# Third layer's self-attention: where the steps of its second half stand in the slots of the loop beside it

## The chip, the cores and the metric

The kernel runs on one core of a Trainium2 chip, in one launch. The metric is the device time of one execution in microseconds (us). A core has five engines that each work through an instruction list of their own in order: TensorE (PE, matrix products), VectorE (DVE), ScalarE (ACT), GpSimd (POOL) and SyncE (SP, which here only starts transfers). They meet through semaphores: an instruction waits until another engine has counted far enough. An instruction that waits holds up everything behind it on its own engine.

## The reference

The input `x` is 16 batch rows of 56 tokens by 256 features; a context of 1500 rows by 128 features goes with each batch row. Four layers run one after the other on `x`, each with attention to the context:

```python
x = L0(x, ctx)                      # one-head attention, a gate, rmsnorm
x = L1(x, ctx, mask)                # layernorm, 16-head cross attention, then a gelu MLP
x = L2(x, ctx, types, positions)    # self-attention, cross attention, then a silu MLP
x = L3(x, ctx, mask)                # as L1, other weights
```

The change is in the self-attention of the third layer (L2). Cut to what matters, with 16 heads of 16 features, and with two sets of weights ("v" and "l") between which a mask `vm` of the tokens chooses:

```python
x = rms_norm(hidden, ln_in_w)
mixed = where(vm, x @ v_qkv, x @ l_qkv)
q, k, v = heads(split(mixed, 3))
q, k = apply_rotary(q, k, position_ids)
p = softmax(where(causal, q @ k.T / 4, lowest))
ctx = p @ v
hidden = hidden + where(vm, ctx @ v_dense, ctx @ l_dense)
ci = rms_norm(hidden, ln_post_cross_w)       # then the cross attention to the 1500 context rows
```

## The kernel before, in words

**Groups and items.** The 16 batch rows make four groups of four (`gi` 0 to 3, `T` = 224 tokens). A layer on a group is an item; `program` runs 16 items in order, `k` = 0 to 15. An item's main loop (`att0`, `att13`, `att2`) does the attention to the context. Everything else (what comes before an item's attention, `pre...`, and after it, `post...`) is written as Python generators that run beside the main loop of another item: the main loop takes a step of the generator now and then, and the instructions of that step are recorded at that place. So `pre2(gi)`, which holds the changed lines, runs beside item `k` = 7 + `gi`: for group 0 beside the last attention of the second layer (`rows`), for groups 1 to 3 beside the cross attention of the third layer (`att2`) of the group before.

**What sets how many steps a slot takes.** A generator yields the TensorE time that its step is worth, or nothing ("an empty turn"). `pace(share, kept, most)` adds `share` to a balance `line["due"]` and takes up to `most` steps while the balance is over `kept`; each step's worth is taken off. An empty turn ends the call at once, and leaves the balance (up to 3.0) for the next one. `pace` returns whether it took a step that was worth something, and `att2` uses that:

```python
weights_pair(b, j)
full = pace(SHARES[gi][line["behind"]], -0.8, 1)
...
if ahead < B and full:
    largest(ahead, n_ahead)
if last >= 0:
    sums_chunk(last, n)
    sums_chunk(last, n + 1)
if ahead < B and not full:
    largest(ahead, n_ahead)
```

A slot of `att2` is one `j` of six for each batch row `b`. In it stand `weights_pair` (L1441 spreads the shifts into four banks, L1450 adds the scores to them; ACT takes the exponentials `pw` out of these banks at L1455, POOL adds them up at L1467), `largest` (L1404, four banks; DVE takes the largest out of each at L1409), `sums_chunk` (L1482), in some slots `own_sums` (L1508), `values` (L1387), `keys` (L1375) or `shifts` (L1417 to L1430), and a second call of `pace` at the end that takes up to two steps.

**The self-attention's steps.** `scores(pr)` makes the scores of half `pr` (two batch rows) in two banks `e`, and ACT takes exponentials into a tile `s`. `weights(pr, e)` divides `s` by its sums, on DVE alone (L1178, L1179, L1180). `turns(pr, e)` turns a tile by 16 small products with the identity (L1188) and copies it on ACT to `turned` (L302). `sums(pr)` needs both tiles of a half: 16 products with `v` (L1205), then ACT's `own` (L302) and DVE's L1216 into `cT`. With both halves done, DVE masks `cT` twice (L1322), and PE multiplies by the two value matrices (L1329, the value product), whose sum DVE adds to `x` (L1335). The squares of `x` follow on ACT (L389), the root and the scaled rows `xn` on POOL (L390, L320, L400), and PE turns `xn` (L310).

**Banks.** Every product but the long sums goes to one ring of seven banks of PSUM, the memory that PE writes to: `ps_s`, tag "sc", `bufs=7`. The tiles take the banks in turn, in the order in which the program asks for them, so a product waits until the reader of the tile seven places earlier is done.

**Order.** The program is recorded in the order of these calls; the tile framework then orders each engine's list, and may move an instruction past others.

Of the kernel before, what the change touches and what calls it, by code (L numbers as in the profile page):

```python
# [62 lines left out]
def tile_kernel(ctx: ExitStack, tc: tile.TileContext, a, layers=4, groups=NG):  # L63
# [18 lines left out]
    def psum(pool, tag):  # L82
        return pool.tile([128, 512], F32, tag=tag, name=tag)
# [5 lines left out]
    def mm():  # L89
        return psum(ps_s, "sc")  # L90
# [1131 lines left out]
    def pre2(gi):  # L1222
# [12 lines left out]
        scores, weights, turns, sums = self_attention(qT, kept, v, cT)  # L1235
# [68 lines left out]
        weights(0, 1)  # L1304
        turns(0, 0)
        yield 1.2
        weights(1, 0)
        turns(0, 1)
        yield 1.2
        weights(1, 1)  # L1310
        sums(0)
        yield 0.7
        turns(1, 0)
        yield 1.2
        turns(1, 1)
# [4 lines left out]
        for n, m in enumerate((vm, nvm)):  # L1320
            mrow = m[:, gi * G : (gi + 1) * G, :].rearrange("p b n -> p (b n)")
            nc.vector.tensor_tensor(  # L1322
                ce[:, n], cT, mrow.unsqueeze(1).to_broadcast([128, 2, T]), ALU.mult
            )
        p = mm()
        for i in range(NT):
            for n in range(2):
# [365 lines left out]
    def program():  # L1693
# [5 lines left out]
        for name in ("L1", "L3"):  # L1699
            parts.append(tuple(partial(f, name) for f in (pre13, first13, att13, post13)))  # L1700
        parts.insert(2, (pre2, first2, att2, None))
        items = [(*parts[l], gi) for l in range(layers) for gi in range(groups)]
        states = {}
# [335 lines left out]
```

## Time and profile before

| what | value |
|---|---|
| three runs | 1436.54, 1442.94, 1444.49 us; median 1442.94 us |
| the profiled execution | 1437.15 us; its span from first to last instruction 1435.3 us |
| busy share of the span | PE 95%, DVE 54%, ACT 52%, POOL 37% |
| mean granted TensorE clock | 0.986 |
| PE idle before L1329, waiting for L1322 | 6.8 us in 4 waits |
| PE idle before L1188, waiting for L1180 | 4.6 us in 3 waits |
| PE idle before L1205, waiting for `turned` | 2.8 us in 2 waits |

The page of the profile gives busy times by engine and by group of instructions; its answers on waits give, for each line of an engine, what it waited for, in total, how often, and at most. A timeline gives the start, the length and the count of each group in order, with the idle time ahead of it in brackets. An fp32 product shows as two records, so 16 products of L1188 are "x32". L302 is the line of a helper that copies on ACT; the tile's name tells which copy it is. The granted clock says at which part of its full speed TensorE ran in a stretch.

### The profile page before, as it was taken

What the parts mean: (1) busy time and instruction counts of PE and PEld (TensorE: products, weight loads), DVE (VectorE), ACT (ScalarE), POOL (GpSimd) and SP (SyncE); (2) the same over time, 40 slices, a digit from 0 to 9 for tenths busy, and PEclk for the clock granted to TensorE, in tenths of its full rate; (3) what the DMA queues carried; (4) which work ended last, traced back from release to release, by engine and by line L of the source; (5) the groups of instructions that cost most, each with busy time, mean ns of one, the idle gap of its engine ahead of it and who ended that gap; (6) DMA issues with size and microseconds to landing.
All of it is one profiled execution on the core that took longest, in us unless ns stands there. A gap on an engine that the chain in (4) does not pass through costs nothing.

```text
span 1435.3 us, 32417 instructions
## 1 busy us (share of the span) xinstructions
PE 1357.3 (95%) x13638; PEld 938.2 (65%) x13638; DVE 777.7 (54%) x1794; ACT 744.8 (52%) x1703; POOL 526.2 (37%) x567
## 2 busy tenths in 40 slices
PE   6989999999899999999999999999899998999998
PEld 4667677775656556655555556656467776877776
DVE  4444754647575754467545755455565445455641
ACT  2334866756543547445554544444356565557661
POOL 0011001010101677767767768788743112100000
PEclk9999999999999999999999999999999999999998
DMA  7853224232322021110201022131122343333320
GB/s 270 351 191 126 85 89 145 90 112 65 103 76 81 23 82 52 54 56 24 81 31 43 29 71 68 52 103 56 39 82 94 134 152 101 124 118 123 108 89 10
DMA packets 38808, 135.78 MB, mean 95 GB/s; under 512 B 8605, under 2 KB 18493, under 8 KB 34557
## 3 DMA queue, kind: packets, MB, share of 16 engines
q1 hardware_dynamic: 33901, 119.03, 24.1%
q0 software_dynamic: 2592, 10.85, 2.2%
q10 hardware_dynamic: 2160, 3.74, 0.8%
q8 instruction: 109, 1.79, 0.5%
q14 instruction: 46, 0.38, 0.1%
HBM read 129.01 MB, written 4.59 MB: 93 GB/s over the span
## 4 chain that ended last, share of the span: by engine, by line
PE 75%; DVE 12%; ACT 6%; POOL 3%; DMA 3%; issue 1%; SPq 0%; DVEq 0%; POOLq 0%; ACTq 0%
PE sc L642 9%; PE sc L624 8%; PE sc L1092 7%; PE sc L1404 7%; PE sc L1450 4%; PE o L1482 4%; PE sc L1642 4%; DVE mx L1409 3%; PE sc L907 3%; PE sc L1120 3%; PE sc L1387 3%; PE sc L1441 3%; PE sc L1661 2%; PE sc L1375 2%; POOL all L1467 2%; ACT p L302 2%
## 5 line engine op out<-in xcount | busy, mean ns | idle before, releaser
L1467 POOL TENSOR_TENSOR all<-all,pw 125x448 f32<-125x448 f32 x300 | 341.1, 1149 | 125.8 <-ACT pw L1455 114.7
L1409 DVE TENSOR_REDUCE mx<-sc 112x1 f32<-112x500 f32 x384 | 233.4, 669 | 140.6 <-PE sc L1404 140.5
L1455 ACT ACTIVATE pw<-sc 125x448 f32<-125x448 f32 x384 | 177.7, 550 | 102.8 <-PE sc L1450 100.1
L631 ACT ACTIVATE p<-p,few 128x384 f32<-128x384 f32 x224 | 136.9, 611 | 99.3 <-DVE few L627 98.9
L624 PE MATMUL sc<-ktl,qa 128*128 128x384 f32 x448 | 176.9, 504 | 0.0
L627 DVE CUSTOM_DVE_ANT_0 p<-sc,mkl 128x384 f32<-128x384 f32 x224 | 121.8, 551 | 92.1 <-PE sc L624 87.4
L642 PE MATMUL sc<-p,kvl 32*128 32x224 f32 x2160 | 149.5, 353 | 4.7 <-DVE qa L940 3.3
L642 PEld LDWEIGHTS sc<-p,kvl 32*128 32x128 f32 x2160 | 136.3, 185 | 20.5 <-issue 9.6
L642 PE MATMUL o<-p,kvl 32*128 32x224 f32 x720 | 144.6, 352 | 0.0
L143 POOL TENSOR_SCALAR mkl<-m32l 128x384 bf16<-128x384 uint8 x32 | 16.3, 510 | 314.1 <-DVE few L627 292.5
L642 PEld LDWEIGHTS o<-p,kvl 32*128 32x128 f32 x720 | 130.7, 185 | 0.0
L302 ACT ACTIVATE p<-p,few 128x384 f32<-128x384 f32 x224 | 121.1, 608 | 8.6 <-DVE few L618 7.2
L1404 PE MATMUL sc<-ck,qs 32*112 32x500 f32 x768 | 122.5, 626 | 2.8 <-ACT ck L302 1.4
L661 DVE STREAM_TRANSPOSE p<-p 128x768 f32<-128x768 f32 (+1 forms) x96 | 102.8, 1095 | 28.6 <-ACT p L302 28.4
L624 PEld LDWEIGHTS sc<-ktl,qa 128*128 128x128 f32 x448 | 78.8, 190 | 37.4 <-issue 9.0
L1450 PE MATMUL sc<-qs,ck 32*125 32x224 f32 x1536 | 98.8, 355 | 0.0
L320 POOL TENSOR_TENSOR stat<-stat,half_less 112x2 f32<-112x2 f32 (+1 forms) x33 | 23.1, 700 | 201.8 <-DVE stat L344 162.0
L302 ACT ACTIVATE ot<-sc 128x224 f32<-128x224 f32 x64 | 32.0, 609 | 121.1 <-PE o L642 83.5
L1482 PE MATMUL o<-pw,vc 125*32 125x224 f32 x1536 | 93.0, 359 | 0.0
L1482 PEld LDWEIGHTS o<-pw,vc 125*32 125x32 f32 x1536 | 40.2, 109 | 69.9 <-issue 57.2
L1450 PEld LDWEIGHTS sc<-qs,ck 32*125 32x125 f32 x1536 | 77.4, 183 | 1.1
L302 ACT ACTIVATE vc<-sc 125x512 f32<-125x512 f32 x48 | 28.6, 596 | 82.0 <-PE sc L1387 79.2
(286 smaller groups left out, 2360.7 us busy)
## 6 DMA issues: line engine op xcount, KB each, us to landing
kvl<-in_ctx_last SPq DMA_DIRECT2D x30, 768.0 KB, 4.2
kt<-in_ctxT SPq DMA_DIRECT2D x23, 750.0 KB, 5.0
w<-in_L_W SPq DMA_DIRECT2D x16, 1024.0 KB, 4.8
w<-in_L_Wq SPq DMA_DIRECT2D x8, 1024.0 KB, 5.0
w<-in_L_Wo SPq DMA_DIRECT2D x8, 1024.0 KB, 5.6
ktl<-in_ctxT SPq DMA_DIRECT2D x32, 192.0 KB, 2.5
w<-in_L_v_qkv SPq DMA_DIRECT2D x4, 768.0 KB, 6.8
w<-in_L_l_qkv SPq DMA_DIRECT2D x4, 768.0 KB, 4.1
```

Of the source, the lines that this page charges most:

```text
L302: nc.scalar.activation(out, in_, AF.Copy, scale=scale)
L624: line["scored"] = nc.tensor.matmul(sc[:, :LW], u["q"][:, i * 128 : (i + 1) * 128], u["kt"], start=True, stop=True).ins.name
L627: line["drained"] = nc.vector.tensor_tensor_reduce(u["p"][:, i], sc[:, :LW], u["mask"], 1.0, -LOWEST, ALU.add, ALU.min, mn[:, i : i + 1],) ...
L631: nc.scalar.activation(u["p"][:, i], u["p"][:, i], AF.Exp, bias=mn[:, i : i + 1], scale=-1.0, accum_out=den[:, i : i + 1],)
L642: product = nc.tensor.matmul(o[g][:, : RB * BW], y["kv"][part, j, :], y["p"][part, :, j * BW : (j + 1) * BW], start=j == 0, stop=j == LB - ...
L661: nc.vector.transpose(blocks, blocks)
L1404: nc.tensor.matmul(banks[g][: 2 * N, :SW], made["q"][part, rows], made["k"][part, cols], start=True, stop=True,)
L1409: line["drained"] = nc.vector.tensor_reduce(made["mx"][:, half * 4 + g, s : s + 1], banks[g][: 2 * N, :SW], AX.X, ALU.max).ins.name
L1450: nc.tensor.matmul(banks[g][:CP, c * QH : (c + 1) * QH], made["k"][part, at : at + CP], made["q"][part], start=False, stop=c == 1, skip_gr ...
L1455: line["weighed"] = nc.scalar.activation(p[:, :, g * QH : (g + 1) * QH], banks[g][:CP, : 2 * QH].rearrange("p (c n) -> p c n", c=2), AF.Ex ...
L1467: added = engine.tensor_tensor(made["all"][:, cols], made["all"][:, cols] if j else p[:, 0, cols], p[:, c, cols], ALU.add,)
L1482: nc.tensor.matmul(made["o"][part, :QH], made["v"][:, n, part], p[:, r * QH : (r + 1) * QH], start=n == 0, stop=n + 1 == NC, skip_group_ch ...
```

## The change

In `pre2`, behind the first turn of the first half, the second half's first weighting `weights(1, 0)` goes and an empty turn stands in its place, ahead of the first half's second turn. Both weightings of the second half come one step later. A second empty turn stands between the halves, behind `weights(1, 1)`, and a third ahead of the value product, behind the two masked copies. No instruction is added or taken away. Line numbers in this document are those of the kernel before; in the changed kernel the lines below the change stand three further down.

```diff
         weights(0, 1)
         turns(0, 0)
         yield 1.2
-        weights(1, 0)
+        yield
         turns(0, 1)
         yield 1.2
-        weights(1, 1)
+        weights(1, 0)
         sums(0)
         yield 0.7
+        weights(1, 1)
+        yield
         turns(1, 0)
         yield 1.2
         turns(1, 1)
...
             nc.vector.tensor_tensor(
                 ce[:, n], cT, mrow.unsqueeze(1).to_broadcast([128, 2, T]), ALU.mult
             )
+        yield
         p = mm()
         for i in range(NT):
             for n in range(2):
```

## The prediction

> **What bounds the kernel now.** The first line of the page's busy part says who sets the time:
>
> ```profile
> PE 1357.3 (95%) x13638; PEld 938.2 (65%) x13638; DVE 777.7 (54%) x1794; ACT 744.8 (52%) x1703; POOL 526.2 (37%) x567
> ```
>
> PE idles only 1435.3 − 1357.3 = 78.0 us. A change that adds and drops no instruction can win only idle time of PE, or time that PE spent at a lower clock. So I read PE's waits next, for the lines that the change moves:
>
> ```profile
> PE sc L1329 <- DVE l L1322: 6.8, 4, 1.8
> PE sc L1188 <- DVE s L1180: 4.6, 3, 1.6
> PE sc L1205 <- ACT turned L302: 2.8, 2, 2.1
> ```
>
> Each row is total, number of waits, longest. They are 14.2 us, 1.0% of the span: the most that could go in waits. L1329 waits once in each group; L1188 once in groups 1 to 3, L1205 twice in group 0 (beside `rows`). The third view is PE's timeline in group 1 (groups 2 and 3 repeat it within 0.1 us, but for the clock):
>
> ```profile
> 498.30 0.93 PE L1450 MATMUL sc<-qs,ck 32*125 32x224 f32 x16
> 500.74 1.14 PE L1188 MATMUL sc<-ident,s 120*64 120x56 f32 x32 [1.51 <-DVE s L1180]
> 501.81 1.11 PE L1404 MATMUL sc<-ck,qs 32*112 32x500 f32 x8
> ...
> 505.21 0.71 PE L1441 MATMUL sc<-shift,ones_r 2*125 2x448 f32 x4
> 505.52 1.16 PE L1450 MATMUL sc<-qs,ck 32*125 32x224 f32 x16
> 506.61 0.61 PE L1205 MATMUL sc<-turned,l 56*32 56x112 f32 x32
> ...
> 517.35 0.61 PE L1205 MATMUL sc<-turned,l 56*32 56x112 f32 x32
> 517.90 0.96 PE L1482 MATMUL o<-pw,vc 125*32 125x224 f32 x16
> 520.52 1.98 PE L1329 MATMUL sc<-w,l 128*112 128x256 f32 x8 [1.66 <-DVE l L1322]
> ```
>
> The reader sees two holes, 1.51 and 1.66 us, and between them dense work. The fourth view, DVE's timeline there, shows who is late:
>
> ```profile
> 500.07 2.09 DVE L1180 TENSOR_TENSOR s<-s,stat 120x448 f32<-120x448 f32 x2
> 502.09 0.60 DVE L1178 TENSOR_REDUCE stat<-s 120x8 f32<-120x448 f32 x1
> 502.73 0.20 DVE L1179 RECIPROCAL stat<-stat 120x8 f32<-120x8 f32 x1
> 502.97 0.68 DVE L1180 TENSOR_TENSOR s<-s,stat 120x448 f32<-120x448 f32 x1
> 503.57 2.42 DVE L1409 TENSOR_REDUCE mx<-sc 112x1 f32<-112x500 f32 x4
> 505.91 0.49 DVE L1514 RECIPROCAL rest<-sc 128x56 f32<-128x56 f32 x1
> ```
>
> DVE has no gap from the weightings to L1409, which empties the four banks of L1404. The last view is the clock by stretches (the number before the last two is the granted clock):
>
> ```profile
> 820.00:821.00 1.00, 0.94 (x20) 0.57 (x13) 1.00 (x3) 0.40 (x1) 0.00 (x0) 1.00 0.00 0
> 821.00:822.00 1.00, 0.00 (x0) 0.00 (x0) 1.00 (x5) 0.95 (x3) 0.00 (x0) 1.00 0.00 0
> 822.00:823.00 1.00, 0.50 (x16) 0.50 (x17) 1.00 (x2) 0.90 (x3) 0.83 (x1) 0.94 0.00 0
> 823.00:824.00 1.00, 1.00 (x22) 0.99 (x19) 1.00 (x2) 0.00 (x0) 0.92 (x2) 0.50 0.00 0
> ```
>
> This is group 3's hole before L1188 (1.56 us): half clock follows. From that turn to L1205 takes 7.16 us (822.50 to 829.66) instead of 5.87 in group 2 (664.29 to 670.16): a price of 1.3 us. In group 0 half clock also follows the holes of 2.13 and 1.82 us, from about 379.3 to 382.7, which costs half of 3.4 = 1.7.
>
> **The change in the order.** The changed program's instruction lists differ from the old ones only at these four places; no transfer moves, on SP or another queue. In groups 1 to 3 DVE's list keeps its order up to the value product, third weighting ahead of L1409, although the call comes later in the source. What moves is PE: the second turn of half 0 goes from ahead of L1404 to behind L1387, a slot's end; L1482 comes ahead of L1404, since an empty turn makes `pace` return false; the turns of half 1 go a piece later, so that the last one stands right ahead of its L1205; L1329 moves behind L1482, L1404, L1424 and L1375. ACT's copies follow their turns. POOL's list changes in groups 1 and 2 alone: the second L320 stands ahead of L400.
>
> **Groups 1 and 2, walked with group 1's times.** PE is free at 499.23. L1482 0.90, L1404 1.04, L1508 0.51, L1387 1.07 end at 502.75, the turn (1.07) at 503.82; its tile is ready at 502.16. The 1.51 us hole is gone here. But the ring of seven banks now gives L1441 exactly the four banks of this slot's L1404; before, it was the turn's and three of them. So its fourth product waits for the fourth L1409, at 505.99, with 0.2 us from DVE's end to PE's start (L1514 ends at 506.40, L1205 starts at 506.61). L1450 (0.86) runs from 506.27 to 507.13, against 506.61 before: **0.5 lost**, the hole having moved two products on. L1455 follows 1.0 us behind the start of L1450 and frees the next L1404's banks; that start moves more than that end, so **0.15 more is lost**. The last turn ends at about 517.97; ACT starts 0.19 later (512.11 to 512.30 shows this), copies in 0.54, and 0.2 us of L1205 and L1441 is there to fill: **0.65 lost** on `turned`, until 518.85. Then **1.66 won**: L1329 needs `own` (0.6), L1216 (0.57) and both L1322 (1.16), 2.5 us behind L1205 with delays, and 4.6 us of L1441, L1450, L1482, L1404, L1424 and L1375 lie between. With L1404's DVE work early, L1441's next wait (0.36) and the stretched L1450 (1.15 for 0.86) go: **0.65 won**. Last, L1335 now ends at 528.45 instead of 526.3: squares 0.91, L390 0.2, L320 0.72, the second L320 0.72, L400 1.83, with delays 533.1, while PE reaches L310 at 531.8. L310 then ends at 533.5 (533.43 before) where PE would have been at 532.3; it had waited little, but the L1441 behind it is no longer stretched: **0.5 lost** net. Sum: −0.5 − 0.15 − 0.65 + 1.66 + 0.65 − 0.5 = 0.5 us won for each.
>
> **Group 3.** No second L320, so the last term halves at least: 0.75 to 1.25, I take 1.0. Its half clock (1.3) came from a hole that is now split up; I count half, 0.65.
>
> **Group 0.** The two L624 between turns and sums change places, and half 1's two turns stand together. L1205's first wait stays near 0.5 (ACT's third exponential, 0.6, now stands ahead of the copy; an L624, 0.85, covers it). The second wait moves, since ACT must first finish eight copies (3.13 + 0.6 + 0.52): `turned` at 375.5 and 376.0 instead of 376.34, 0.5 us won. The value product starts at 378.85, as before (378.80), because an L627 (0.55) now stands ahead of L1322 on DVE; but one L624 (0.9) is done by then, that used to stand among L1329. Behind it all 0.35 is won if half clock follows as before, 2.05 if not. PE idles 3.65 of the 5.2 us before, so I give half clock two in three: 0.95.
>
> **What no row of before prices** is whether half clock follows the new hole at L1441 (2.1 us with 0.3 of work in it). Bounds: 0, and 1.3 to 1.7 for each of groups 1 to 3. The nearest rows are the six holes of 1.51 to 1.66 us there, one of which was followed by it; for a longer one I take one in three, 3 × 1.5 / 3 = 1.5 lost.
>
> The Trainium skill ("TensorE: Matmul & The Clock Gate", section "Why this matters for your kernels") has throughput drop only behind idle gaps over some 3 us. The 1.56 us gap above, with 0.50 behind it, disagrees, and the trace decides. By that rule the 1.5 would be left out, and 1.5 more won.
>
> **Sum.** 0.95 + 2 × 0.5 + 1.0 + 0.65 − 1.5 = 2.1 us won. Against its own execution: 1437.15 − 2.1 = 1435.05. That execution is 5.8 below the median of the runs; against the median, 1442.94 − 2.1 = 1440.8. The runs spread over 8 us, so 0.5% (7.2) is about what a measurement tells from no change.
>
> **The rivals.**
> - *The holes simply go* (faster). Had L1441 other banks to write, or DVE done L1409 earlier, 14.2 us of waits and 3.0 of clock would go: 1442.94 − 17.2 = 1425.7; with group 0's waits mostly kept, near 1433. For it: PE is the bound, and what covers L1329 is long. Against: DVE is gapless to 505.99. Chance 0.13.
> - *The new hole costs the clock* (slower). The place is L1441 behind L1409 in groups 1 to 3: 0.5 + 0.15 + 0.65 + up to 1.7 of half clock = 3.0 each, 9.0 in all, 1452, if L1329's gain is eaten at L310. It decides from 2.4 us a group (7.2 / 3). For it: half clock behind 1.56 us. Against: five like holes without. Chance 0.11.
> - *Nothing moves.* The ordering takes instructions across calls, as DVE's list shows; then 1442.9. Against it: PE's list does differ. It ends within 0.5% too, and shares the 0.76 of the forecast.
>
> **Range and chances.** The forecast's own range is 1435.7 to 1450.2 by the bound of 0.5%. The terms' bounds are 1442.94 − 9 (all clock terms won, waits as summed, near 1434) and + 4.5 (half clock in all three groups with the 0.5 won lost). With 2 us of scatter on each side: 1432 to 1449. Faster 0.13, within 0.5% 0.76, slower 0.11.
>
> **What would show it.** Right: L1188 waits for L1180 no more, L1329 for L1322 in group 0 alone (about 1.5 us); new rows of L1441 on L1409, of L1205 on `turned` (0.65 in groups 1 to 3) and of L310 on POOL's `xn` (about 1 us in groups 1 and 2). Wrong: L1441 without a wait, or L1409 earlier than the weightings. It fails if clock windows fall otherwise than counted, each 1.3 to 1.7 us, here or elsewhere.

## The result, and the profile after

The changed kernel is slower: 1444.22 us median (1438.66 to 1450.07, 20 runs) against 1438.55 us (1434.03 to 1444.49, 20 runs), a ratio of 1.0035 with a 95% interval from 1.0021 to 1.0050. The forecast was 2.1 us faster. The profiled execution took 1446.13 us, its span 1444.3 us, at a mean granted clock of 0.975 (0.986 before).

The busy part of the page, and the rows of PE's waits that answer to those of before (a line of the changed kernel below the change is three higher: L1441 is L1444, L1404 is L1407, L1409 is L1412, L1329 is L1332; L1322 stands ahead of the last empty turn and is L1324):

```profile
PE 1374.4 (95%) x13638; PEld 947.9 (66%) x13638; DVE 779.1 (54%) x1794; ACT 746.5 (52%) x1703; POOL 526.1 (36%) x567
```

```profile
PE sc L1205 <- ACT turned L302: 2.2, 3, 1.5
PE sc L1444 <- DVE mx L1412: 1.8, 4, 0.5
PE sc L310 <- POOL xn L400: 1.6, 3, 0.6
PE sc L1332 <- DVE l L1324: 1.2, 1, 1.2
```

PE waits less: 1444.3 − 1374.4 = 69.9 us idle instead of 78.0. L1188's wait for L1180 (4.6 us) is gone from the list, L1332's is 1.2 instead of 6.8. But PE is busy for 17 us more with the same 13638 products. The same products last longer where the clock is halved. PE's timeline of group 1 shows one such place:

```profile
505.10 1.14 PE L1390 MATMUL sc<-l2w,kt 128*125 128x128 f32 x8
506.17 1.14 PE L1188 MATMUL sc<-ident,s 120*64 120x56 f32 x32
507.75 2.22 PE L1444 MATMUL sc<-shift,ones_r 2*125 2x448 f32 x4 [0.44 <-DVE mx L1412]
509.50 1.22 PE L1453 MATMUL sc<-qs,ck 32*125 32x224 f32 x16
510.65 0.61 PE L1205 MATMUL sc<-turned,l 56*32 56x112 f32 x32
511.19 2.92 PE L1407 MATMUL sc<-ck,qs 32*112 32x500 f32 x8
514.04 1.72 PE L1485 MATMUL o<-pw,vc 125*32 125x224 f32 x16
515.69 2.07 PE L1390 MATMUL sc<-l2w,kt 128*125 128x128 f32 x8
517.69 0.65 PE L1444 MATMUL sc<-shift,ones_r 2*125 2x448 f32 x4
...
524.57 0.46 PE L1444 MATMUL sc<-shift,ones_r 2*125 2x448 f32 x1
525.05 0.59 PE L1205 MATMUL sc<-turned,l 56*32 56x112 f32 x24
```

From the end of the turn (507.31) to the start of L1453 (509.50) pass 2.2 us, in which PE has nothing but the four products of L1444, 0.31 us of work in the kernel before (505.21 to 505.52). They come one at a time, although the list of waits puts only 0.44 of that down as idle. DVE's timeline says what they wait for: the third weighting stands ahead of L1412, which empties their banks.

```profile
503.54 2.09 DVE L1180 TENSOR_TENSOR s<-s,stat 120x448 f32<-120x448 f32 x2
505.55 0.60 DVE L1178 TENSOR_REDUCE stat<-s 120x8 f32<-120x448 f32 x1
506.19 0.20 DVE L1179 RECIPROCAL stat<-stat 120x8 f32<-120x8 f32 x1
506.43 0.67 DVE L1180 TENSOR_TENSOR s<-s,stat 120x448 f32<-120x448 f32 x1
507.03 2.42 DVE L1412 TENSOR_REDUCE mx<-sc 112x1 f32<-112x500 f32 x4
```

The stretches of the same execution, with the granted clock as the third number from the right:

```profile
509.00:510.00 1.00, 0.88 (x13) 0.59 (x17) 0.97 (x3) 0.00 (x0) 0.29 (x1) 1.00 0.00 0
510.00:511.00 1.00, 1.00 (x43) 0.71 (x37) 0.11 (x1) 0.36 (x1) 0.00 (x0) 1.00 0.00 0
511.00:513.00 2.00, 2.00 (x31) 1.38 (x12) 0.23 (x1) 1.98 (x6) 1.22 (x2) 0.57 0.00 0
513.00:515.00 2.00, 2.00 (x17) 0.59 (x16) 2.00 (x5) 0.00 (x0) 2.00 (x2) 0.50 0.03 8
515.00:517.00 2.00, 2.00 (x17) 1.31 (x7) 0.68 (x2) 0.00 (x0) 1.25 (x2) 0.50 0.00 0
517.00:518.00 1.00, 1.00 (x8) 0.77 (x11) 0.00 (x0) 0.20 (x1) 0.00 (x0) 0.50 0.00 0
```

Half clock starts within 2 us behind the hole and lasts some 6.8 us: L1485 takes 1.72 instead of 0.96, L1390 2.07 instead of the 1.14 of the slot before.

### The profile page after: what moved, and what is told of

Read it like the earlier page. It is cut to its first block, busy times and chain, and to the rows that moved or that the text cites. A ratio compares the mean times of both kernels' runs of the same rounds, so it can differ in the third digit from the quotient of the medians.

```text
span 1444.3 us, 32417 instructions
## 1 busy us (share of the span) xinstructions
PE 1374.4 (95%) x13638; PEld 947.9 (66%) x13638; DVE 779.1 (54%) x1794; ACT 746.5 (52%) x1703; POOL 526.1 (36%) x567
## 5 line engine op out<-in xcount | busy, mean ns | idle before, releaser
L1412 DVE TENSOR_REDUCE mx<-sc 112x1 f32<-112x500 f32 x384 | 233.2, 669 | 144.0 <-PE sc L1407 143.9
L1407 PE MATMUL sc<-ck,qs 32*112 32x500 f32 x768 | 123.6, 634 | 2.8 <-ACT ck L302 1.4
L1453 PE MATMUL sc<-qs,ck 32*125 32x224 f32 x1536 | 100.7, 361 | 0.0
L1485 PE MATMUL o<-pw,vc 125*32 125x224 f32 x1536 | 94.8, 365 | 0.0
L1485 PEld LDWEIGHTS o<-pw,vc 125*32 125x32 f32 x1536 | 40.7, 110 | 70.5 <-issue 58.1
L1453 PEld LDWEIGHTS sc<-qs,ck 32*125 32x125 f32 x1536 | 78.9, 187 | 1.3
L1020 DVE COPY ot<-sc 128x224 f32<-128x224 f32 x32 | 18.2, 568 | 99.0 <-PE o L642 84.9
```

Of the source, the lines that this page charges most:

```text
L1407: nc.tensor.matmul(banks[g][: 2 * N, :SW], made["q"][part, rows], made["k"][part, cols], start=True, stop=True,)
L1412: line["drained"] = nc.vector.tensor_reduce(made["mx"][:, half * 4 + g, s : s + 1], banks[g][: 2 * N, :SW], AX.X, ALU.max).ins.name
L1453: nc.tensor.matmul(banks[g][:CP, c * QH : (c + 1) * QH], made["k"][part, at : at + CP], made["q"][part], start=False, stop=c == 1, skip_gr ...
L1485: nc.tensor.matmul(made["o"][part, :QH], made["v"][:, n, part], p[:, r * QH : (r + 1) * QH], start=n == 0, stop=n + 1 == NC, skip_group_ch ...
```

## The experiments

**Two ways of counting.** Each run comes with its span and its mean granted clock. I split a span into (1 − clock) × span, the part lost to a lower clock, and the rest. And in each profile I read the granted clock us by us, and counted how many stretches of 3.4 us at half clock fall into each group, from the last products of L1155 (second half's scores) to L1343. Both tables stand here; the edits follow. Means of a kernel's timed runs (the 20 runs of the kernel before that belong to the result have no clock on record, so its rows are from the two later sessions):

| kernel | runs | span, us | clock | lost to clock, us | rest, us |
|---|---|---|---|---|---|
| before | 25 | 1438.9 | 0.9827 | 24.9 | 1414.1 |
| before, in the later session | 17 | 1439.7 | 0.9825 | 25.2 | 1414.6 |
| changed | 20 | 1443.0 | 0.9759 | 34.8 | 1408.2 |
| without the value product's empty turn | 10 | 1441.0 | 0.9803 | 28.4 | 1412.6 |
| value product's empty turn alone | 10 | 1442.6 | 0.9793 | 29.9 | 1412.7 |
| changed, weightings behind L1409 | 4, and 6 in the later session | 1429.9, 1431.6 | 0.9837, 0.9808 | 23.2, 27.4 | 1406.7, 1404.1 |
| that, without the value product's turn (later session) | 6 | 1434.3 | 0.9828 | 24.6 | 1409.7 |
| changed, second turn made twice | 10 | 1440.8 | 0.9788 | 30.6 | 1410.3 |
| changed, second turn made three times (later session) | 10 | 1435.7 | 0.9841 | 22.8 | 1412.8 |

Sessions differ a little: in the session of the result the mean times of the two kernels lie 6.0 us apart, the spans of the first and the third row only 4.1. So a difference between rows of different sessions holds to some 2 us.

Lengths of groups 0, 1, 2, 3 in us, and stretches at half clock in each:

| profile | lengths | half clock |
|---|---|---|
| before, three profiles | 43.44 42.33 42.37 43.47; 44.00 42.35 42.36 43.52; 44.07 42.35 42.36 43.46 | 1 0 0 1; 2 0 0 1; 2 0 0 1 |
| changed, three profiles | 42.37 44.32 43.96 41.87; 42.35 44.30 43.91 43.45; 40.66 44.38 43.96 43.44 | 1 2 2 1; 1 2 2 2; 0 2 2 2 |
| without the value product's turn | 42.72 45.00 42.30 44.27 | 1 2 0 2 |
| value product's turn alone | 43.18 42.24 43.80 43.40 | 1 0 1 1 |
| weightings behind L1409, two profiles | 42.35 39.48 39.48 38.91; 43.29 39.48 39.48 38.93 | 1 0 0 0; 2 0 0 0 |
| that, without the value product's turn | 42.73 40.05 40.24 39.65 | 1 0 0 0 |
| second turn made twice | 42.35 41.53 41.58 45.34 | 1 0 0 3 |
| second turn made three times | 40.70 41.59 41.57 41.05 | 0 0 0 0 |

**Where a hole lies.** In each of these thirteen profiles the stretches at half clock begin on one grid of 3.413 us, from the first to the last to within 0.01 us. In the changed kernel's first profile those of groups 0 to 3 begin at 381.57, 511.28, 675.12 and 835.54 us, which are 38, 48 and 47 steps apart. The grid divides holes of one kind into those that half clock follows and those that it does not:

| hole | profiles | followed by half clock when it begins so many us behind a grid point | not followed |
|---|---|---|---|
| before L1188, 1.50 to 1.56 us | three of before, one with the value product's turn alone | 1.47 to 1.68 (4 holes) | 0.31 to 1.01, and 1.96 (8 holes) |
| at L1441, 2.2 to 2.3 us with 0.3 us of work in it | three of changed, one without the value product's turn | 0.07 to 1.36, and 2.74 to 3.15 (11 holes) | 2.23 (1 hole) |

No run moved the grid on purpose, so this is read off and not tested, and why a hole has nearly the same place on it in every profile of one kernel stays open.

**The theories.** Mine, once I had seen the profile after: L1441's new wait behind L1409 makes PE nearly idle for 2 us in each of groups 1 to 3, and half clock follows there. Rivals: the later value product costs the time (through L310's wait for POOL); or the stretches fall by chance, elsewhere.

**More profiles of both kernels**, unchanged.

> The kernel before, unchanged, for another profile. If half clock is brought by holes inside groups 1 to 3: none to two stretches of 3.4 us at half clock there (at most one a group), and as many as in the changed kernel, give or take three, in the rest of the span. If the stretches come from elsewhere: the counts in groups 1 to 3 of both kernels agree within one, and those in the rest differ.

> As the look before it: none to two stretches at half clock in groups 1 to 3 by the theory of the hole.

> The changed kernel, unchanged, for another profile. Theory of the hole: three to six stretches of 3.4 us at half clock in groups 1 to 3, each beginning within 5 us behind the third slot's L1441, and the rest of the span as in the kernel before, give or take three. Otherwise none to two there.

> As the look before it: three to six stretches at half clock in groups 1 to 3 by the theory of the hole.

Measured: 1438.58 and 1438.92 us for the kernel before, 1441.79 and 1440.52 for the changed one, one run each. The second table's first two rows are as clear as the theory asks: groups 1 to 3 hold one stretch in every profile of before, always in group 3, and five, six and six in the changed kernel, the first of a group beginning at most 4.1 us behind the start of the hole. The rest of the span holds 11, 14 and 15 of them before and 17, 14 and 11 in the changed kernel, the same in the mean within one. Over the four groups the changed kernel is longer by 172.99 − 172.03 = 0.96 us (means of three). The 93.3 us between groups 0 and 1 hold one more stretch in two of its three profiles and none in before's (1.05 us in the mean); the stretches between the later groups are 0.2 us longer each. The rest of the difference of these profiles, 2.2 us, lies ahead of the first changed instruction: of the six, that part took 353.3 to 359.0 us with the same code, and holds two to four stretches. That is chance, and it is the noise of every single run here. So these profiles place some 2.4 us of the 5 to 6 us that the result measures in the changed stretch and between the groups (0.96, 1.05 and twice 0.2); where the others arise they do not show.

**Weightings behind L1409.** On DVE alone, the second half's weightings are ordered behind the L1409 recorded last; the lists of PE, ACT, POOL and SP are the changed kernel's. Not shown below: `gi` is handed to the function.

```diff
         def weights(pr, e):
             _, s = state["s", pr, e]
             den = stat(8)[:PR]
-            nc.vector.tensor_reduce(den, s, AX.X, ALU.add)
+            summed = nc.vector.tensor_reduce(den, s, AX.X, ALU.add)
+            if pr and gi:
+                behind(summed, line["drained"], "banks go first")
```

> The changed kernel, with both weightings of the second half ordered behind the L1409 of the slot before on DVE in groups 1 to 3; every other engine's list is as in the changed kernel. Clock theory: L1441 finds its banks free, its wait (2 us) and the half clock behind it go: 3 to 4.5 us less a group, 1430 to 1436 us, faster than both kernels. If the clock windows are set elsewhere (by chance, or by stages that the change does not touch), only the 0.6 us goes by which the hole is longer than the one it replaced: 1441 to 1444 us.

Measured: 1431.85 us (1429.63 to 1433.97, 4 runs), ratio to the kernel before 0.9917 (0.9894 to 0.9941). DVE's timeline, then PE's at the same place (L1182 is L1180 here, L1414 is L1409; of PE's lines L1190 is L1188, L1446 is L1441, L1455 is L1450, L1207 is L1205 and L1409 is L1404):

```profile
504.51 0.62 DVE L1182 TENSOR_TENSOR s<-s,stat 120x448 f32<-120x448 f32 x1
506.03 2.43 DVE L1414 TENSOR_REDUCE mx<-sc 112x1 f32<-112x500 f32 x4 [0.90 <-PE sc L1409]
508.38 0.61 DVE L1178 TENSOR_REDUCE stat<-s 120x8 f32<-120x448 f32 x1
```

```profile
507.54 1.14 PE L1190 MATMUL sc<-ident,s 120*64 120x56 f32 x32
508.61 0.47 PE L1446 MATMUL sc<-shift,ones_r 2*125 2x448 f32 x4
508.92 0.93 PE L1455 MATMUL sc<-qs,ck 32*125 32x224 f32 x16
509.78 0.61 PE L1207 MATMUL sc<-turned,l 56*32 56x112 f32 x32
510.32 2.19 PE L1409 MATMUL sc<-ck,qs 32*112 32x500 f32 x8
```

The four products now take 0.31 us, and no stretch at half clock is left in groups 1 to 3: each is 3.0 to 4.8 us shorter than in the changed kernel's first profile. So the order on DVE alone decides over the hole and what follows it. This kernel beats both. Timed again:

> The changed kernel with the weightings of the second half behind L1409, as in the first run of this edit, timed more often. If the gain is the edit's: 1429 to 1434 us again, ratio to the kernel before 0.990 to 0.995, and no half clock in groups 1 to 3. If the first run was lucky with its clock: a ratio of 0.996 or more.

Measured: 1432.57 us (1432.00 to 1438.39, 6 runs), ratio 0.9943 (0.9923 to 0.9962). The lengths of groups 1 and 2 are the same to 0.01 us. The ratio is less good; these runs lost 27.4 us to the clock instead of 23.2, and the profile has none of that in groups 1 to 3.

**Work put into the hole.** This edit separates the clock from the wait: the wait's end stays where DVE puts it, and PE is kept busy up to it, by making the second turn of half 0 twice (the same 16 products into the same bank again, 1.07 us a group).

```diff
-            for j in range(8):
+            for j in range(16 if gi and (pr, e) == (0, 1) else 8):
+                j = j % 8
```

> The changed kernel, in which the second turn of half 0 is made twice in groups 1 to 3 (the same 16 products again, 1.07 us more PE work a group, right ahead of the wait of L1441). Clock theory: the added work lies in the hole and costs nothing, and keeps half clock away in some groups: 1438 to 1443 us, less than the changed kernel though it does more, with fewer half-clock windows in groups 1 to 3. Otherwise: the added work costs between 0 and 3.2 us, 1444 to 1447 us.

Measured: 1444.15 us (1433.37 to 1447.42, 10 runs), ratio 1.0009 (0.9985 to 1.0034). The added 3.2 us of work cost nothing that shows, but the time is above the 1438 to 1443 that I had expected of the theory, just inside the 1444 to 1447 of its rival. Its profile shows groups 1 and 2 free of half clock, and 2.8 and 2.4 us shorter than in the changed kernel; but a hole of about 1 us is left at L1441 (its four products take 1.4 us instead of 0.31, in all three groups alike), and group 3 has three stretches behind it. It begins there 0.17 us behind a grid point, in groups 1 and 2 at 0.67 and 3.05. With 24 in place of 16, the hole is full:

> The changed kernel, in which the second turn of half 0 is made three times in groups 1 to 3 (2.14 us more PE work a group, as long as the hole). Theory of the hole: no hole is left at L1441, no half clock in groups 1 to 3, each of them 41.5 to 43 us long, shorter than in the changed kernel (43.4 to 44.4) although it does more; 1437 to 1443 us. If half clock does not come from the hole: 1446 to 1451 us.

Measured: 1437.46 us (1431.38 to 1441.99, 10 runs), ratio 0.9973 (0.9958 to 0.9989). PE's timeline and the clock in group 1 (L1189 is L1188 here, L1445 is L1441, L1454 is L1450, L1206 is L1205, L1408 is L1404):

```profile
502.61 3.01 PE L1189 MATMUL sc<-ident,s 120*64 120x56 f32 x96
505.54 0.90 PE L1445 MATMUL sc<-shift,ones_r 2*125 2x448 f32 x4
505.98 1.22 PE L1454 MATMUL sc<-qs,ck 32*125 32x224 f32 x16
507.13 0.61 PE L1206 MATMUL sc<-turned,l 56*32 56x112 f32 x32
507.68 2.00 PE L1408 MATMUL sc<-ck,qs 32*112 32x500 f32 x8
```

```profile
506.00:508.00 2.00, 2.00 (x54) 1.52 (x53) 0.56 (x2) 1.12 (x4) 0.00 (x0) 1.00 0.03 8
508.00:510.00 2.00, 2.00 (x16) 0.82 (x16) 0.76 (x3) 1.46 (x5) 1.75 (x2) 1.00 0.00 0
510.00:512.00 2.00, 2.00 (x29) 1.50 (x24) 2.00 (x4) 0.33 (x1) 1.92 (x3) 1.00 0.00 0
```

With 6.4 us more PE work than the changed kernel it is faster than that kernel and than the one before. The first table says why: it loses 22.8 us to the clock instead of 34.8, while the rest is 4.6 us longer. The price of half clock in groups 1 to 3 is the difference of their lengths to this kernel's: 2.74, 2.37 and 1.87 us (means of the changed kernel's three profiles), 7.0 us together.

**The parts of the change.**

```diff
 (changed kernel)
-        yield          # ahead of the value product
```

> The change without its empty turn ahead of the value product. Clock theory (the changed kernel is slower because L1441 now waits behind L1409 in groups 1 to 3, about 2 us with little work, and half clock follows there): the hole stays, so it stays slower than the kernel before, 1442 to 1447 us, and half clock shows within 5 us behind the third slot's L1441 in at least two of groups 1 to 3. Value-product theory (the later value product makes L310 wait for POOL's rows and costs the time): back to 1437 to 1440 us.

Measured: 1442.56 us (1438.92 to 1447.76, 10 runs), ratio 1.0007 (0.9988 to 1.0025). The hole at L1441 stays in all three groups. Two stretches each follow it in groups 1 and 3, as many groups as the clock theory asks, but none in group 2. PE's timeline in groups 1 and 2 (L1443 is L1441, L1406 is L1404, L1484 is L1482):

```profile
502.06 2.22 PE L1443 MATMUL sc<-shift,ones_r 2*125 2x448 f32 x4 [0.45 <-DVE mx L1411]
505.67 2.75 PE L1406 MATMUL sc<-ck,qs 32*112 32x500 f32 x8
508.35 1.72 PE L1484 MATMUL o<-pw,vc 125*32 125x224 f32 x16
```

```profile
668.39 2.22 PE L1443 MATMUL sc<-shift,ones_r 2*125 2x448 f32 x4 [0.45 <-DVE mx L1411]
671.84 2.00 PE L1406 MATMUL sc<-ck,qs 32*112 32x500 f32 x8
673.77 0.96 PE L1484 MATMUL o<-pw,vc 125*32 125x224 f32 x16
```

The same hole stands in both, and only that of group 1 is followed by half clock (L1484 takes 1.72 us there and 0.96 in group 2): the hole of group 2 is the one that begins 2.23 us behind a grid point. So the hole alone does not always bring half clock; where it lies decides as well. The ratio's interval has 1 in it, so that this kernel is slower than the one before is not shown; it lies nearer to that one than to the changed kernel. And the other way round:

```diff
 (kernel before)
+        yield          # ahead of the value product, alone
```

> The kernel before with the empty turn ahead of the value product alone. Clock theory: no wait of L1441 behind the weightings is made, so not slower than before: 1435 to 1440 us. Value-product theory: 1441 to 1446 us, with the wait of L310 for POOL's rows in groups 1 and 2.

Measured: 1445.28 us (1440.79 to 1447.23, 10 runs), ratio 1.0018 (1.0002 to 1.0035). Here my theory missed: this kernel has no new hole at L1441 and is slower all the same. It waits 1.4 us less and loses 5.0 us more to the clock than the kernel before (first table). Its profile shows the old hole before L1188 in group 2, which was never followed by half clock in the kernel before, followed by it now: it begins 1.68 us behind a grid point, where it began at 0.31 to 0.46. Is the later value product bad in itself? Without it, in the kernel whose weightings stand behind L1409:

> The kernel with the weightings behind L1409, without the empty turn ahead of the value product. If that empty turn costs 3 to 4 us by itself (it did so in both places where it was tried alone or left out), 1426 to 1430 us. If it only cost by where clock stretches fell, and otherwise covers the wait for L1322 (0.7 us a group without it): the same or slower than with it, 1431 to 1435 us.

Measured: 1435.70 us (1434.32 to 1438.92, 6 runs), ratio 0.9955 (0.9939 to 0.9971), against 1432.57 with it in the same session. Its groups 1 to 3 are 0.57, 0.76 and 0.72 us longer. So in this kernel the later value product is no cost: it covers what it should cover. In the other two places it lost more to the clock than it won, which fits a move of the later holes against the grid. That is argued and not shown: one profile of each shows the stretches in groups 1 to 3 (above), and 13 and 17 more in the rest of the span, where chance alone moves them by several.

## Why the prediction was wrong

**The order and the waits: right.** The walk gave L1441 its banks from the fourth L1409, 0.5 us late; measured: ahead of the hole L1450 starts 3.48 us later than before (501.78 against 498.30), so L1205 would start at 506.61 + 3.48 = 510.09; it starts at 510.65, 0.56 late. The hole of L1188 is gone, L1329's is gone in groups 1 to 3 and 1.2 us in group 0 (forecast 1.5). `turned` holds L1205 up to 525.05 in group 1, some 0.4 us (0.65). L310 waits 0.6, 0.6 and 0.4 in groups 1 to 3 (1.0 in two). Group 0 won 2.0 us in the mean where the sum has 0.95 (its own values and chances make 0.92): its stretches at half clock fell from 1, 2 and 2 to 1, 1 and 0, and more than the forecast gave to the order is, as far as three profiles show, luck. Group 3 won only 0.6 (1.65), since it has half clock still, now behind the new hole. In all, the span without what the clock took fell by 5.9 us (first table).

**The clock: the step that failed.** It is the sentence "for a longer one I take one in three, 3 × 1.5 / 3 = 1.5 lost". In the changed kernel the hole brings half clock in all three groups and in every profile, in groups 1 and 2 for two stretches in a row: 7.0 us instead of 1.5. Both the chance and the length of one stretch a group were too low. I had treated the six holes of before as six draws, one of which hit. But the three profiles of before show the same group hit every time: what decides there is the place on the grid, for which the sum has no term, and six holes of 1.5 us say little on one of 2.2. With this term, groups 1 to 3 together should have become 1.15 us shorter; they became 3.0 us longer (131.2 against 128.2, means of three profiles). Over the whole span, the loss to the clock rose by 9.9 us (34.8 − 24.9) against 5.9 us won. The prediction had named what would make it fail: clock windows that fall otherwise than counted.

**The rival that came true** is the second one, "the new hole costs the clock", at its place; its price was 3.0 us a group for hole and clock, and it was given 0.11. It did not reach its bound of 0.5% since the waits won elsewhere, L1329's above all, were kept. "The holes simply go" is what the edit on DVE makes of the change: 0.6 to 0.8% faster than before, where the forecast had given 0.13 to more than 0.5%.

The Trainium skill ("TensorE: Matmul & The Clock Gate", section "Why this matters for your kernels"), which asks for no idle gap over some 3 us between bursts of products, would have left even the 1.5 us out. The runs speak against that figure at this place: holes of 2.2 us with 0.3 us of work in them were followed by half clock eleven times in twelve, holes of 1.5 us four times in twelve.

## What to carry to other kernels

A hole in TensorE's work is not priced by its length alone: where a profile shows half clock behind holes of 1.5 us, moving a hole or joining it with another may cost several us, and the granted clock belongs next to the waits in the first reading. A change that shifts later work may also move old holes to a worse or a better place, so the sign of a small change should not be read from one profile. With a ring of banks, a step that is moved on one engine hands other banks to everything behind it; look for who empties those, and whether work that isn't urgent stands ahead of it. Here one ordering on DVE, urgent emptying before weightings that are needed a slot or two later, turned a change that cost 0.35% into one that wins 0.6 to 0.8%.

## What was not expected of the hardware

- Useless work made a kernel faster: 96 products more than the changed kernel's, 6.4 us of TensorE time, gave a ratio to the kernel before of 0.9973 (0.9958 to 0.9989) where the changed kernel has 1.0035 (1.0021 to 1.0050). With 48 products, 3.2 us, it is 1.0009, but the intervals overlap.
- Half clock comes in stretches of 3.41 us or a multiple, on one grid through each execution, and for the same hole in the same place in every profile: group 3 of the kernel before in three of three, groups 1 and 2, with holes of the same lengths, in none.
- In the first 356 us, which no kernel here changes, the time until group 0 spreads from 352.9 to 361.8 us over all profiles, with two to four stretches at half clock.
